# Layer 2's first normalisation in a four-layer kernel: sums of chunks 1 and 2 moved beside the first 1/std, the reciprocal in halves, seven loads in one queue

## The chip, the cores and the metric

The kernel runs on one core of a Trainium2 chip. A core has TensorE for matrix products (PE, and PEld for its loads of weights), VectorE (DVE), ScalarE (ACT) and GpSimd (POOL) for elementwise work, and SyncE (SP), which here only issues DMAs; POOL and ACT can issue DMAs too. Each engine works through its own list of instructions in order and waits on semaphores for the others. The metric is the device time of one execution in microseconds (us).

## The reference

The input x has 256 x 256 places of 128 channels. Four layers follow each other, each of the form x = x + f(gn(x)), where gn normalises groups of 4 channels over all places. Cut to what matters here:

```
# layer 1: a, b from sigmoids of products; triangle product; g * (ln(z) @ Wz + bz)
x = x + L1(gn(x))
# layer 2
zn = layernorm(gn(x))                      # over the 128 channels of each place
a = sigmoid(zn @ Wga + bga) * (zn @ Wla + bla)
b = sigmoid(zn @ Wgb + bgb) * (zn @ Wlb + blb)
k = einsum('bimc,bmjc->bijc', a, b)
x = x + sigmoid(zn @ Wgo + bgo) * (layernorm(k) @ Wlo + blo)
```

Layer 0 is a triangle attention, layer 3 a pair of small convolutions in each direction. All is in float32.

## The kernel before, in words

Activations lie in DRAM with the channels on the 128 partitions and the 65536 places along the row: `xT`, `x1T`, `x2T`, `x3T` after the layers. The places are cut into 32 chunks of `SC` = 2048, each of four pieces of `CK` = 512. Lists of instructions are as written within the blocks marked `manual_schedule`; between the blocks, instructions that touch different data may be put ahead of others of the same engine.

**Layer 1's last loop** (pool `p4`, lines 1063 to 1148) takes the 32 chunks in the order `order4`; in what follows a number between 0 and 31 in layer 1 is a place in this order. For each place, PE makes a product of the normalised z (`p4_pz`, L1116) into PSUM, which has room for one chunk only, and PE and ACT make the gate four places ahead (`gate4`, L1089 and L1092). DVE forms (pz + bz) * gate and its sum (L1126). The result is added to x either by POOL in one instruction (L1137) or, for the places in `by_dve`, by DVE in two (L1133); in that case the product stays in PSUM until the addition is done. ACT then takes the sum of squares of the new chunk (`sum4`, L1099), one place later, and SP stores it to `x2T` (L1143). `fetch_z` loads z through POOL's queue every fourth place (L1075).

**Statistics of layer 2** (lines 1155 to 1182). DVE reduces the sums, PE spreads them over groups of channels, ACT takes the square root (`gn2_sd`, L208), and DVE makes the scales: `r2`, `slide2` (a sliding column that sums channels, times r2), `mr2neg`, `wf2`, `off2`.

**Layer 2's first stage** (pool `p5`, lines 1203 to 1334). Seven chunks are loaded ahead (`load5`, L1211): chunks 0 to 3 by POOL's queue, 4 to 6 by SP's. For the layer norm over channels, ACT squares a chunk (`square5`, L1216), and PE sums the chunk and its square over channels with one-column weights (`sums5`, L1229): a group of four matmuls for x and a group of four for the squares, each on a quarter of the columns of the array; each matmul shows as two in the trace. ACT squares the mean (L1235), DVE subtracts (L1237) and clips (L1248), ACT takes the root (L1249), DVE the reciprocal. The first time this is done for chunk 0 alone: its reciprocal (L1283) is spread over the partitions by four matmuls (`broadcast_rows`, L1191) and chunk 0 is normalised by DVE from PSUM (L1290). Then it is done for chunks 1 to 3 together (`sums5(1, KB)`, L1229; reciprocal L1294), stored as a row in DRAM (L1222) and read back spread over the partitions, chunk by chunk (`spread5`, L1261). The loop over the 32 chunks (L1297) then makes four products per chunk (`product5`, L1272), two sigmoids (L1307) and two gated products (L1311), with the squares and sums for the next block of four chunks between them. PSUM pool `psM` has three buffers for the products and for the broadcast, `psX` one for the sums.

Later come layer 2's products over 128 channels (`p6`), its output (`p7`) and layer 3.

Of the kernel before, what the change touches and what calls it, by code (L numbers as in the profile page):

```python
# [8 lines left out]
F32 = mybir.dt.float32  # L9
AF = mybir.ActivationFunctionType  # L10
ALU = mybir.AluOpType
# [4 lines left out]
P = 128  # L16
# [3 lines left out]
SC = 2048  # L20
NSC = T // SC
CK = 512
# [9 lines left out]
def kernel(ctx: ExitStack, tc: tile.TileContext, a: dict, out: bass.AP):  # L32
    nc = tc.nc
# [17 lines left out]
    x2T = rows("x2T", D)  # L51
# [18 lines left out]
    const = ctx.enter_context(tc.tile_pool(name="const", bufs=1, reuse_waits="tile"))  # L70
# [30 lines left out]
    epst = const.tile([P, 1], F32, name="epst")  # L101
# [51 lines left out]
    sel = const.tile([P, 32], F32, name="sel")  # L153
# [69 lines left out]
    slide = const.tile([P, 63], F32, name="slide")  # L223
# [23 lines left out]
    with tc.tile_pool(name="x0", bufs=1, reuse_waits="tile") as xres, tc.tile_pool(name="p0", bufs=3, reuse_waits="tile") as sb:  # L247
# [14 lines left out]
        with tc.tile_pool(name="p0ps", bufs=3, space=PSUM, reuse_waits="tile") as ps, tc.tile_pool(name="f0ps", bufs=2, space=PSUM, reuse_waits="tile") as fps, tc.tile_pool(name="f0", bufs=1, reuse_waits="tile") as wk, tc.manual_schedule():  # L262
# [90 lines left out]
            for i, s in enumerate(order0):  # L353
                xt = xts.pop(s)
                xc = hold(s) if s < HELD else sb.tile([P, SC], F32, name="p0_xc", tag="xs")
                for c in range(2):
# [8 lines left out]
                    xh = xc[c] if isinstance(xc, tuple) else xc[:, c * GT : (c + 1) * GT]  # L365
# [71 lines left out]
        with tc.tile_pool(name="p1", bufs=3, reuse_waits="tile") as wk_sb, tc.tile_pool(name="p1ps", bufs=3, space=PSUM, reuse_waits="tile") as ps, tc.tile_pool(name="p1pt", bufs=2, space=PSUM, reuse_waits="tile") as psT, tc.tile_pool(name="p1mm", bufs=3, space=PSUM, reuse_waits="tile") as psP:  # L437
# [7 lines left out]
            with tc.manual_schedule():  # L445
                prs, trs, turned, sqs = {}, {}, {}, {}
# [152 lines left out]
    xs = {}  # L599
# [10 lines left out]
    with tc.tile_pool(name="p2e", bufs=6, reuse_waits="tile") as eb, tc.tile_pool(name="p2c", bufs=1, reuse_waits="tile") as cs:  # L610
        with tc.tile_pool(name="p2u", bufs=2, reuse_waits="tile") as sb, tc.tile_pool(name="p2S", bufs=2, space=PSUM, reuse_waits="tile") as psS, tc.tile_pool(name="p2z", bufs=1, space=PSUM, reuse_waits="tile") as psZ, tc.tile_pool(name="p2M", bufs=3, space=PSUM, reuse_waits="tile") as psM, ExitStack() as by_hand:
# [163 lines left out]
            for t_ in range(2):  # L775
                lo = 0 if t_ else 32
# [154 lines left out]
    with x1_scope, far_scope:  # L931
# [132 lines left out]
        with tc.tile_pool(name="p4", bufs=3, reuse_waits="tile") as sb, tc.tile_pool(name="p4psg", bufs=2, space=PSUM, reuse_waits="tile") as psg, tc.tile_pool(name="p4psz", bufs=2, space=PSUM, reuse_waits="tile") as psz, tc.manual_schedule():  # L1064
            zs, gts, sums = {}, {}, []
            junk = sb.tile([P, SC], F32, name="p4_junk", bufs=1)

            order = order4
            by_dve = (5, 11, 17, 23, 29, NSC - 1)

            def fetch_z(i):
                if i < NSC:
                    zs[i] = sb.tile([P, 2, CK], F32, name="p4_z", bufs=2)
                    for m in range(2):
                        (nc.gpsimd if i > 4 else nc.sync).dma_start(  # L1075
                            zs[i][:, m, :],
                            znD.rearrange("k (j b t) -> b j k t", j=8, t=CK)[order[i + 2 * m] % 16],
                        )

            def gate4(i):  # L1080
                if i < NSC:
                    xt = xs[order[i]]
                    tag, bufs = ("g", 3) if i % 7 < 3 else ("Z", 4)
                    gts[i] = gate_pool.tile([P, SC], F32, name="p4_g", tag=tag, bufs=bufs)
                    for h in range(2):
                        pg = psg.tile([P, 2, CK], F32, name="p4_pg")
                        for c in range(2):
                            k = 2 * h + c
                            nc.tensor.matmul(  # L1089
                                pg[:, c, :], lhsT=wgf, rhs=xt[:, k * CK : (k + 1) * CK], start=True, stop=True  # L1090
                            )
                        nc.scalar.activation(  # L1092
                            gts[i][:, h * 2 * CK : (h + 1) * 2 * CK], pg.rearrange("p c t -> p (c t)"),
                            AF.Sigmoid, bias=bgf,
                        )

            def sum4():
                i = sums.pop(0)
                nc.scalar.activation(  # L1099
                    junk, xs[order[i]], AF.Square, bias=c1neg, accum_out=qsum[:, i : i + 1]  # L1100
                )

            LEAD = 4
            fetch_z(0)
            fetch_z(4)
            for i in range(7):
                gate4(i)
            for i, s in enumerate(order):
                xt = xs[s]
                if i > 1 and i % 4 == 1:  # L1110
                    fetch_z(i + 3)
                half, z = s // 16, zs[i - i % 4]
                pz = [psz.tile([P, 2, CK], F32, name="p4_pz") for _ in range(2)]
                for c in range(4):
                    q = slice(32 * c, 32 * c + 32)
                    nc.tensor.matmul(  # L1116
                        pz[c // 2][:, c % 2, :], lhsT=wz4[q, half, :], rhs=z[q, (i // 2) % 2, :],
                        start=True, stop=True,
                    )
                if i + LEAD > 6:  # L1120
                    gate4(i + LEAD)
                gt = gts.pop(i)
                for h in range(2):
                    hs = slice(h * 2 * CK, (h + 1) * 2 * CK)
                    pzh = pz[h].rearrange("p c t -> p (c t)")
                    nc.vector.scalar_tensor_tensor(  # L1126
                        pzh if i in by_dve else gt[:, hs], pzh, bz, gt[:, hs], ALU.add, ALU.mult,
                        accum_out=usum[:, 2 * i + h : 2 * i + h + 1],
                    )
                if i in by_dve:  # L1130
                    for h in range(2):
                        hs = slice(h * 2 * CK, (h + 1) * 2 * CK)
                        nc.vector.tensor_tensor(  # L1133
                            xt[:, hs], pz[h].rearrange("p c t -> p (c t)"), xt[:, hs], ALU.add
                        )
                else:
                    nc.gpsimd.tensor_tensor(xt, xt, gt, ALU.add)  # L1137
                sums.append(i)
                if len(sums) > 1:
                    sum4()  # L1140
                if i:
                    s_ = order[i - 1]
                    nc.sync.dma_start(x2T[:, s_ * SC : (s_ + 1) * SC], xs[s_])  # L1143
                j = i - 4 + SLOTS
                if i > 3 and j < NSC:
                    load1(order[j], home[order[j - SLOTS]])
            sum4()
            nc.sync.dma_start(x2T[:, s * SC : (s + 1) * SC], xt)
# [16 lines left out]
    m2, r2 = gn_groups(mv2, "gn2")  # L1165
    wf2 = const.tile([P, 5, D], F32, name="wf2")
    nc.vector.tensor_scalar(wf2, w2[:, 0:5, :], r2, None, ALU.mult)
    slide2 = const.tile([P, 63], F32, name="slide2")
# [15 lines left out]
    H2 = 2 * CK  # L1184

    def broadcast_rows(psX, rows, s, name, tag="x"):


        rb = [psX.tile([P, 2, CK], F32, name=name, tag=tag) for _ in range(2)]
        for c in range(4):  # L1190
            nc.tensor.matmul(  # L1191
                rb[c // 2][:, c % 2, :], lhsT=sel[32 * c : 32 * c + 32, s : s + 1].to_broadcast([32, P]),
                rhs=rows[32 * c : 32 * c + 32, :], start=True, stop=True,
            )
        return [t.rearrange("p c t -> p (c t)") for t in rb]
# [7 lines left out]
    KB = 4  # L1203
    BT = KB * SC
    with tc.tile_pool(name="p5", bufs=2, reuse_waits="tile") as sb, tc.tile_pool(name="p5q", bufs=4, reuse_waits="tile") as sq_pool, tc.tile_pool(name="p5psX", bufs=1, space=PSUM, reuse_waits="tile") as psX, tc.tile_pool(name="p5psM", bufs=3, space=PSUM, reuse_waits="tile") as psM, tc.manual_schedule():
        xs, sqs, zns, vars_ = {}, {}, {}, {}

        def load5(s):
            if s < NSC:
                xs[s] = x_pool.tile([P, SC], F32, name="p5_x", tag="x")  # L1210
                (nc.gpsimd if s < KB else nc.sync).dma_start(xs[s], x2T[:, s * SC : (s + 1) * SC])  # L1211

        def square5(s):
            if s < NSC:
                sqs[s] = sq_pool.tile([P, SC], F32, name="p5_sq")
                nc.scalar.activation(sqs[s], xs[s], AF.Square, bias=mr2neg, scale=r2)  # L1216

        def store_block(dram_row, lo, hi, t):

            by_c = dram_row.rearrange("o (s c t) -> c (o s) t", c=4, t=CK)  # L1220
            for c in range(4):
                nc.sync.dma_start(by_c[c, lo:hi, :], t[32 * c + lo : 32 * c + hi, :])  # L1222

        def sums5(lo, hi):
            st = psX.tile([P, 2, CK], F32, name="p5_st")
            for s in range(lo, hi):
                for i, (w, src) in enumerate(((slide2, xs[s]), (slide, sqs[s]))):
                    for c in range(4):
                        nc.tensor.matmul(  # L1229
                            st[32 * c : 32 * c + 32, i, :], lhsT=w[:, 31 - s : 63 - s],  # L1230
                            rhs=src[:, c * CK : (c + 1) * CK], start=(s == lo), stop=(s == hi - 1),
                        )
                del sqs[s]
            mean2 = sb.tile([P, CK], F32, name="p5_m2", bufs=1)
            nc.scalar.activation(mean2, st[:, 0, :], AF.Square, bias=off2)  # L1235
            var = sb.tile([P, CK], F32, name="p5_var")
            nc.vector.tensor_tensor(var, st[:, 1, :], mean2, ALU.subtract)  # L1237
            return var
# [38 lines left out]
        for s in range(7):  # L1277
            load5(s)

        square5(0)  # L1280
        var = sums5(0, 1)
        root5(var)
        nc.vector.reciprocal(var, var)  # L1283
        store_block(rs2D, 0, 1, var)
        for s in range(1, KB):
            square5(s)
        zns[0] = sb.tile([P, SC], F32, name="p5_zn", bufs=3)
        for h, rb in enumerate(broadcast_rows(psM, var, 0, "p5_pm", tag="p5_pm")):
            hs = slice(h * H2, (h + 1) * H2)
            nc.vector.scalar_tensor_tensor(zns[0][:, hs], xs[0][:, hs], m2, rb, ALU.subtract, ALU.mult)  # L1290
        del xs[0]
        var = sums5(1, KB)
        root5(var)
        nc.vector.reciprocal(var, var)  # L1294
        store_block(rs2D, 1, KB, var)
# [771 lines left out]
```

## Time and profile before

| | us |
|---|---|
| median of 3 runs | 3239.55 (3238.77 to 3243.01) |
| the profiled execution | 3240.66 |
| its span, first to last instruction | 3238.9 |
| busy in the span: PE | 3052.9 (94%) |
| DVE | 2263.2 (70%) |
| ACT | 2034.6 (63%) |
| POOL | 1739.0 (54%) |

Layer 1's last loop runs in the trace from about 1624 to 1781 us, the opening of layer 2 from 1781 to 1811, its loop over chunks from there to about 2230. Times in the timeline are counted from the first instruction of the span. A line of the timeline gives the start, the length from the first start to the last end, engine, line, operation, what is written and read, the count of instructions merged into it, and in brackets how long the engine had been idle before and what released it.

### The profile page before, as it was taken

Reading aid. Unit: us, or ns where it says so; the run is one execution under the profiler, and the core shown is the slowest. Engines: PE = TensorE matmul, PEld = TensorE weight load, DVE = VectorE, ACT = ScalarE, POOL = GpSimd, SP = SyncE. Lnnn points to the kernel's source line nnn. Section 1 sums busy time; section 2 is a strip of 40 time slices with the busy share of each in tenths; the row PEclk is TensorE's granted clock in tenths of the full one; section 3 lists DMA queues with packets and bytes.
Section 4 is the critical chain, followed back from the end, with each engine's and each line's share of the span. In section 5 each row is a group of like instructions: output and inputs, shape, how many; then the busy total and the mean of one; then the engine's idle time right before and its main releaser. Section 6 shows DMA issues by size and latency. Waiting matters only on the chain. (4 is left out here: it accounts for less than half of the span.)

```text
span 3238.9 us, 51714 instructions
## 1 busy us (share of the span) xinstructions
PE 3052.9 (94%) x19908; PEld 1633.7 (50%) x19908; DVE 2263.2 (70%) x2630; ACT 2034.6 (63%) x2274; POOL 1739.0 (54%) x948
## 2 busy tenths in 40 slices
PE   5699999999999999998798899999999989969998
PEld 4535555555555555552533344444699933324444
DVE  5657888888888888884456454445455588858886
ACT  3576777777777777764477544443344457757776
POOL 4005777777777777771277000000255568848887
PEclk8799999999999999999999899999999999989999
DMA  9982333333333333349589677676799989976775
GB/s 372 384 317 95 106 117 118 110 113 119 113 112 120 113 106 121 117 153 420 177 313 401 232 304 296 225 284 238 280 352 351 338 324 389 389 281 197 234 235 153
DMA packets 289527, 746.19 MB, mean 230 GB/s; under 512 B 68473, under 2 KB 139019, under 8 KB 240987
## 3 DMA queue, kind: packets, MB, share of 16 engines
q1 hardware_dynamic: 277313, 720.27, 62.1%
q0 software_dynamic: 8544, 20.34, 1.7%
q8 instruction: 160, 2.62, 0.3%
q10 hardware_dynamic: 3416, 2.19, 0.3%
q14 instruction: 94, 0.77, 0.1%
HBM read 455.26 MB, written 287.45 MB: 229 GB/s over the span
## 5 line engine op out<-in xcount | busy, mean ns | idle before, releaser
L679 POOL TENSOR_TENSOR p_es<-p_e 128x1024 f32<-128x1024 f32 x256 | 603.0, 2366 | 321.2 <-DMA p_x<-xT 197.4
L669 DVE TENSOR_TENSOR p_e<-p_S,tri_raw 128x1024 f32<-128x1024 f32 x512 | 609.0, 1211 | 143.5 <-PE p_S L659 143.4
L677 ACT ACTIVATE p_e<-p_e,mbT 128x1024 f32<-128x1024 f32 x512 | 552.1, 1137 | 62.0 <-DVE p_e L669 61.9
L1272 PE MATMUL p_pm<-p_zn,wf 128*128 128x512 f32 x1040 | 448.7, 593 | 1.9 <-ACT p_a L1307 1.9
L644 PE MATMUL p_mm<-p_xn,w 128*128 128x512 f32 x764 | 404.4, 612 | 0.0
L1272 PEld LDWEIGHTS p_pm<-p_zn,wf 128*128 128x128 f32 x1040 | 196.8, 190 | 253.9 <-issue 247.0
L659 PE MATMUL p_S<-p_qk 32*128 32x256 f32 x4096 | 295.5, 400 | 3.3 <-DVE p_e L669 3.3
L1369 POOL MEMSET k<- 128x512 f32 x1 | 0.5, 527 | 520.8 <-PE p_pm L1272 520.8
L659 PEld LDWEIGHTS p_S<-p_qk 32*128 32x128 f32 x4096 | 186.0, 184 | 159.2 <-PE p_mm L635 91.7
L2025 PE MATMUL tp_z<-p_B,tp_at 128*128 128x256 f32 x1024 | 250.5, 388 | 1.0 <-DMA p_B<-bD 0.7
L692 PE MATMUL p_o<-p_e,p_vg 128*32 128x256 f32 x4096 | 248.8, 383 | 0.0
L626 POOL TENSOR_TENSOR p_xn<-p_xn,p_rs 128x1024 f32<-128x1024 f32 x62 | 148.7, 2398 | 181.1 <-DMA p_rb<-rzD 102.2
L1400 POOL TENSOR_TENSOR k<-k,p_sq 128x512 f32<-128x512 f32 x128 | 163.1, 1274 | 136.4 <-ACT p_sq L1398 136.4
L2025 PEld LDWEIGHTS tp_z<-p_B,tp_at 128*128 128x128 f32 x1024 | 185.1, 191 | 23.6 <-DVE tp_at L2016 1.7
L1399 DVE TENSOR_TENSOR k<-tp_z,k 128x512 f32<-128x512 f32 x128 | 88.6, 692 | 127.2 <-ACT p_sq L1398 127.2
L644 PEld LDWEIGHTS p_mm<-p_xn,w 128*128 128x128 f32 x764 | 125.1, 190 | 103.7 <-issue 87.3
L692 PEld LDWEIGHTS p_o<-p_e,p_vg 128*32 128x32 f32 x4096 | 120.3, 110 | 110.4 <-ACT p_vg L650 41.5
L650 ACT ACTIVATE p_vg<-p_mm,bgh 128x512 f32<-128x512 f32 x128 | 87.9, 687 | 135.2 <-PE p_mm L644 135.2
L1396 ACT COPY p_K<-tp_z 128x512 f32<-128x512 f32 x128 | 75.0, 586 | 155.1 <-PE tp_z L2025 155.1
L1311 DVE SCALAR_TENSOR_TENSOR p_b<-p_pm,b2w,p_b 128x1024 f32<-128x1024 f32 x64 | 82.1, 1283 | 123.7 <-PE p_pm L1272 109.6
L635 PEld LDWEIGHTS p_mm<-w,p_xn 128*128 128x128 f32 x1016 | 133.8, 192 | 61.3 <-issue 60.6
L648 ACT ACTIVATE p_qk<-p_mm,cqkg 128x512 f32<-128x512 f32 x127 | 87.2, 687 | 122.6 <-PE p_mm L644 122.3
(409 smaller groups left out, 6089.2 us busy)
## 6 DMA issues: line engine op xcount, KB each, us to landing
p_x<-x2T SPq DMA_DIRECT2D x60, 1024.0 KB
x<-x1T SPq DMA_DIRECT2D x47, 1024.0 KB
p_x<-in_x_dram SPq DMA_DIRECT2D x32, 1024.0 KB
p_x<-xT SPq DMA_DIRECT2D x64, 512.0 KB
p_rs<-rsD SPq DMA_DIRECT2D x64, 512.0 KB
x2T<-x SPq DMA_DIRECT2D x32, 1024.0 KB
aD<-p_a SPq DMA_DIRECT2D x32, 1024.0 KB
bD<-p_b SPq DMA_DIRECT2D x32, 1024.0 KB
```

The costliest lines, as they stand in the source:

```text
L626: nc.gpsimd.tensor_tensor(xn, xn, groups[g]["rs"], ALU.mult)
L635: nc.tensor.matmul(pm[:, k * D : (k + 1) * D], lhsT=t["xn"][:, b * P : (b + 1) * P], rhs=wf[:, 2 * D : 3 * D], start=True, stop=True,)
L644: nc.tensor.matmul(pm, lhsT=w, rhs=t["xn"][:, cs_], start=True, stop=True)
L659: nc.tensor.matmul(Ss[h // 2][:, h % 2, u, :], lhsT=t["k"][hp, r * N + u * P : r * N + (u + 1) * P], rhs=t["q"][hp, r * N : (r + 1) * N], ...
L669: nc.vector.tensor_tensor(e[:, :, 2 * p : 2 * p + 2, :].rearrange("p u h n -> p h u n"), Ss[p], triT[:, 2 * p : 2 * p + 2, :, :], ALU.add,)
L677: nc.scalar.activation(e[:, u, :, :], e[:, u, :, :], AF.Exp, bias=mbT[:, u, i : i + 1])
L679: nc.gpsimd.tensor_tensor(es, e[:, 0, :, :], e[:, 1, :, :], ALU.add)
L692: nc.tensor.matmul(t["o"][hp, r % 2, :], lhsT=t["v"][:, r * 2 + u, hp], rhs=e[:, u, h, :], start=(u == 0), stop=(u == 1),)
L1272: nc.tensor.matmul(pm[:, c, :], lhsT=wf2[:, i, :], rhs=zns[s][:, k * CK : (k + 1) * CK], start=True, stop=True)
L1399: nc.vector.tensor_tensor(k1, pz, k1, ALU.add)
L1400: nc.gpsimd.tensor_tensor(k2, k2, sq, ALU.add)
L2025: nc.tensor.matmul(pz[:, t, :], lhsT=at[:, u, t * P : (t + 1) * P], rhs=Bc[:, u, :], start=(u == 0), stop=(u == 1))
```

## The change

- `by_dve` goes from places 5, 11, 17, 23, 29, 31 to 4, 10, 16, 22, 27, 31.
- At place 28 ACT gets a small square root that nobody reads; the load of the square root's table, which stood ahead of `gn2_sd`, is placed there with it.
- All seven first loads are issued by POOL. Chunk 0's load stands ahead of the last addition of layer 1 in POOL's list, the other six after it; before it was one, then three, and three on SP.
- `sums5` is cut into `part5` (one group of four matmuls) and `close5` (from the squared mean on). Chunk 0's sums go to a buffer of `psM`.
- ACT's list is now square 0, square 1, squared mean of chunk 0, root, squares 2 and 3; before it was square 0, squared mean, root, squares 1 to 3.
- PE's list is now chunk 0's two groups, chunk 1's two, chunk 2's x, the broadcast in eight matmuls of 256 columns, chunk 3's x, chunk 2's squares, chunk 3's squares. Before, all six groups of chunks 1 to 3 stood after the broadcast, which was four matmuls of 512 columns.
- The reciprocal of chunk 0 is two instructions of 256 columns, and its normalisation four of 512 elements per partition in place of two of 1024.

No other engine's list changes in any other place.

```diff
-            by_dve = (5, 11, 17, 23, 29, NSC - 1)
+            by_dve = (4, 10, 16, 22, 27, NSC - 1)
...
+                if i + LEAD == NSC:
+                    nc.scalar.activation(const.tile([P, 1], F32, name="root_b"), epst, AF.Sqrt)
...
-                (nc.gpsimd if s < KB else nc.sync).dma_start(xs[s], x2T[:, s * SC : (s + 1) * SC])
+                (nc.gpsimd if s < 7 else nc.sync).dma_start(xs[s], x2T[:, s * SC : (s + 1) * SC])
...
+        def part5(st, s, lo, hi, i):
+            w, src = ((slide2, xs[s]), (slide, sqs[s]))[i]
+            for c in range(4):
+                nc.tensor.matmul(
+                    st[32 * c : 32 * c + 32, i, :], lhsT=w[:, 31 - s : 63 - s],
+                    rhs=src[:, c * CK : (c + 1) * CK], start=(s == lo), stop=(s == hi - 1),
+                )
...
-        square5(0)
-        var = sums5(0, 1)
+        for s in range(2):
+            square5(s)
+        st0 = psM.tile([P, 2, CK], F32, name="p5_pm")
+        st1 = psX.tile([P, 2, CK], F32, name="p5_st")
+        for i in range(2):
+            part5(st0, 0, 0, 1, i)
+        var = close5(st0)
         root5(var)
-        nc.vector.reciprocal(var, var)
+        for s in range(2, KB):
+            square5(s)
+        part5(st1, 1, 1, KB, 0)
+        part5(st1, 1, 1, KB, 1)
+        part5(st1, 2, 1, KB, 0)
+        zns[0] = sb.tile([P, SC], F32, name="p5_zn", bufs=3)
+        rb = [psM.tile([P, 2, CK], F32, name="p5_pm") for _ in range(2)]
+        Q = CK // 2
+        for w in range(2):
+            ws = slice(w * Q, (w + 1) * Q)
+            nc.vector.reciprocal(var[:, ws], var[:, ws])
+            for c in range(4):
+                nc.tensor.matmul(
+                    rb[c // 2][:, c % 2, ws], lhsT=sel[32 * c : 32 * c + 32, 0:1].to_broadcast([32, P]),
+                    rhs=var[32 * c : 32 * c + 32, ws], start=True, stop=True,
+                )
         store_block(rs2D, 0, 1, var)
-        for s in range(1, KB):
-            square5(s)
-        zns[0] = sb.tile([P, SC], F32, name="p5_zn", bufs=3)
-        for h, rb in enumerate(broadcast_rows(psM, var, 0, "p5_pm", tag="p5_pm")):
-            hs = slice(h * H2, (h + 1) * H2)
-            nc.vector.scalar_tensor_tensor(zns[0][:, hs], xs[0][:, hs], m2, rb, ALU.subtract, ALU.mult)
+        for h in range(2):
+            for w in range(2):
+                ws = slice(w * Q, (w + 1) * Q)
+                xh, zh = (
+                    t.rearrange("p (c t) -> p c t", t=CK)[:, 2 * h : 2 * h + 2, ws] for t in (xs[0], zns[0])
+                )
+                nc.vector.scalar_tensor_tensor(zh, xh, m2, rb[h][:, :, ws], ALU.subtract, ALU.mult)
         del xs[0]
-        var = sums5(1, KB)
+        part5(st1, 3, 1, KB, 0)
+        part5(st1, 2, 1, KB, 1)
+        part5(st1, 3, 1, KB, 1)
+        for s in range(KB):
+            del sqs[s]
+        var = close5(st1)
         root5(var)
```

More of the change, by code (lines that the diff above doesn't have):

```diff
@@ L1226, in sums5, with close5 @@
             for s in range(lo, hi):
[L1227 to L1232, printed above, removed]
+                part5(st, s, lo, hi, 0)
+                part5(st, s, lo, hi, 1)
                 del sqs[s]
+            return close5(st)
+        def close5(st):
             mean2 = sb.tile([P, CK], F32, name="p5_m2", bufs=1)
```

## The prediction, on record before the result

> **What bounds the kernel now.** I read the page first (PE busy 94% of the span), then the table by stretches, then the timeline, engine by engine, from 1760 to 1812 us, where the edited lines run, then the waits and the landings of the first loads. The page's chain does not reach back this far, so the local chain is followed by hand.
>
> The table of stretches: columns are length, busy time (and count) of PE, PEld, DVE, ACT, POOL, then PE clock, DMA share, GB/s.
> ```profile
> 1782.00:1795.00 13.00, 5.33 (x26) 2.09 (x30) 5.73 (x9) 7.90 (x7) 0.00 (x0) 0.50 1.01 405
> 1795.00:1811.00 16.00, 14.12 (x69) 4.37 (x70) 7.25 (x6) 8.49 (x8) 0.00 (x0) 0.86 0.27 111
> 1811.00:2230.00 419.00, 419.00 (x1308) 176.38 (x1308) 206.35 (x156) 198.45 (x163) 0.00 (x0) 1.00 0.70 262
> ```
> From 1811 PE never stops for 419 us: whatever the opening of layer 2 saves or loses moves all that follows. In 1782 to 1795 PE is busy for 5.33 of 13 us, at half clock, and DMA is full.
>
> The timeline of layer 1's end (POOL) and of the opening (ACT, DVE, PE): start, length, idle before and its releaser.
> ```profile
> 1763.88 4.53 POOL L1137 TENSOR_TENSOR x<-x,p_g 128x2048 f32<-128x2048 f32 x1 [0.64 <-DVE p_g L1126]
> 1768.34 0.58 POOL L1211 DMA_DIRECT2D p_x<-x2T  x1
> 1772.39 4.49 POOL L1137 TENSOR_TENSOR x<-x,p_g 128x2048 f32<-128x2048 f32 x1 [3.46 <-DVE p_g L1126]
> 1776.83 1.61 POOL L1211 DMA_DIRECT2D p_x<-x2T  x3
> ...
> 1779.04 2.00 ACT L1099 ACTIVATE p_junk<-x,c1neg 128x2048 f32<-128x2048 f32 x1
> 1781.16 1.28 ACT L208 ACT_TABLE_LOAD   x1
> 1782.48 0.26 ACT L208 ACTIVATE gn_sd<-gn_pv,epst 128x1 f32<-128x1 f32 x1
> 1783.84 2.09 ACT L1216 ACTIVATE p_sq<-p_x,mr2neg,gn_rstd 128x2048 f32<-128x2048 f32 x1 [1.10 <-DVE mr2neg L1173]
> 1788.62 0.69 ACT L1235 ACTIVATE p_m<-p_st,off 128x512 f32<-128x512 f32 x1 [2.68 <-PE p_st L1229]
> 1795.95 2.09 ACT L1216 ACTIVATE p_sq<-p_x,mr2neg,gn_rstd 128x2048 f32<-128x2048 f32 x1 [0.68 <-DMA p_x<-x2T]
> ...
> 1791.33 3.35 DVE L1283 RECIPROCAL p_var<-p_var 128x512 f32<-128x512 f32 x1 [0.79 <-ACT p_var L1249]
> ...
> 1786.62 1.93 PE L1229 MATMUL p_st<-p_sq,slide 128*32 128x512 f32 x8
> 1794.74 2.09 PE L1191 MATMUL p_pm<-p_var,sel 32*128 32x512 f32 x8 [6.19 <-DVE p_var L1283]
> 1796.76 1.94 PE L1229 MATMUL p_st<-p_x,slide 128*32 128x512 f32 x8
> 1799.88 1.03 PE L1229 MATMUL p_st<-p_x,slide 128*32 128x512 f32 x8
> 1803.41 5.42 PE L1272 MATMUL p_pm<-p_zn,wf 128*128 128x512 f32 x12
> 1810.72 1.55 PE L1272 MATMUL p_pm<-p_zn,wf 128*128 128x512 f32 x3 [1.89 <-ACT p_a L1307]
> ...
> DMA to landing us min/median/max: 9.1/11.4/17.9
> ```
> The path: POOL's last add (to 1776.88), two sums on ACT (to 1781.14), the group deviation (1782.48), square and sums of chunk 0, mean squared (1788.62), root, reciprocal (to 1794.68), broadcast, then six groups of sums of chunks 1 to 3 (1796.76 to 1803.41). From their end, root, a square, the sigmoid's table and the first sigmoid free PE at 1810.72, 7.3 us later. The six groups stand behind a reciprocal that they do not need: PE idles 6.19 us.
>
> [...] a group starts every 1.71 us (1796.76 to 1798.47), later every 0.86 (1799.88 to 1800.74). [...] The loads issued on POOL landed 9.1 to 17.9 us after issue while DMA was full; [...]
>
> **The change, part by part.**
>
> *Layer 1's last chunks* (numbers are places in its order). Until chunk 26 each group of six still has one chunk added by DVE; moved by one, it costs PE the same stall (chunks follow at 4.97 and 5.90 us instead of 4.70 after chunk 23), so nothing. At the end DVE adds 27 instead of 29. DVE has room at 1758.6, and its 2.35 us end at 1760.9, before the products of 28 are ready (1761.3): free. But POOL now adds 28, 29, 30 in a row: from 1763.88, two in 9.06 us, then the load's issue (0.58, 0.07 of it overlapped), then 4.49: end 1777.94 against 1776.88. Chunk 31 on DVE ends some 4 us earlier and gains nothing, as its sum is last on ACT. **+1.06 us** on the path.
>
> *Sqrt table earlier.* Its old load ended at 1782.44, when the matmul it waited with ended too (gn_sd at 1782.48): it saves 0.03. At its new place, before the sum of chunk 27, the next sum that matters waits for POOL until 1768.44: 0, and 1.3 us only if that cover went.
>
> *Chunk 1's square ahead of chunk 0's mean squared.* The group deviation is now at 1783.54, square 0 ends at 1787.0, its four matmuls at 1789.0 (1.93 and a hop; chunk 0's other sums no longer wait for off2 and are done). Square 1 (2.09) fits there if chunk 1 has landed by 1786.9. Its load issues at 1777.94; with the 9.1 us of before it lands at 1787.0. Mean squared then starts at **1789.2, +0.6** on before: 0.4 less than the +1.06, as PE's queue is shorter. Behind square 1 on ACT stand mean squared, root and all that waits for them, so each us later than 1786.9 costs 1 us.
>
> *One queue.* Chunks 4 to 6 leave SP's queue for POOL's (three issues of about 0.55 us, nothing of POOL's behind them until layer 2's products of channels). SP keeps the stores of 30 and 31, 2 MB. So chunk 1 shares with these first; 2 and 3 no longer share with 4 to 6. Bounds for chunk 1 from its issue to landing: [...] 13.4, which chunk 2 took before in second place; so mean squared at 1789.0 to 1793.4. I take the 9.1 that chunk 1 took before in the same crowd. Chunks 2 and 3 follow at some 2.6 us each, by about 1793; squares 2 and 3, after the root, end by 1796.5: hidden.
>
> *Reciprocal in halves.* Two of 256 columns cost the same 3.35 plus about 0.05; the last half ends at mean squared + 6.1 = 1795.3. The first half's broadcast lies under the second; the last four matmuls of 256 columns cost half of 2.09: 1796.35. Four normalising pieces of 512 elements (0.69 each, the PSUM subtraction of that size) end near 1798: under the sums.
>
> *Three groups of sums move ahead of the broadcast* (chunk 1's two, chunk 2's first), into the 6.19 us in which PE idled. Three stay after it: cold 3 x 1.71, warm 3 x 0.86. PE will have been busy from 1787 to about 1793, then idle some 2 us around the broadcasts, so it may be cold again. I take cold, cold, warm: 4.3 us, end 1800.7. Before: 1803.41. **Gain 2.7 us**; ends 1.9 (all cold) and 5.0 (all warm). From there the chain to the second sigmoid is unchanged, and so is chunk 1's row of 1/std (stored, spread and normalised by 1818.9, hardly ahead of PE): it moves along.
>
> Sum: span 3238.9 - 2.7 = 3236.2; the profiled execution lies 1.76 over its span (3240.66), so 3237.96; the median of the runs is 1.11 below that execution: **3236.8**.
>
> **Rivals.**
> *Warm PE:* the clock holds through the broadcasts, the three groups take 2.6. For: three groups more keep PE busy. Against: at 1767.6 PE was cold after 2.6 us idle. 5.0 us, 3234.5; 6.1 if layer 1's end also costs nothing.
> *Late chunk 1 (slower):* square 1 blocks ACT in front of mean squared. Two stores and six loads crowd the queues. It decides where chunk 1 lands after about 1789.6 (11.7 us from issue), when the 2.7 are gone; at the 13.4 us that chunk 2 took before, mean squared starts at 1793.4, loss 1.5, 3241; at 17.9 us, loss 6.0, 3245.5. Against: chunk 1 is first in its queue.
> *Nothing arrives:* the opening shrinks, but chunk 1's spread row is late by as much (its normalisation ended only some 0.4 us before PE wanted it), or a window of PE's clock falls worse: 3239.5. That the order itself does not change is excluded: the built instruction order shows it.
>
> **How the numbers follow.** Forecast 0.45 (own range 3234.5 to 3239), warm 0.25, late 0.15, nothing 0.15. 0.2% is 6.5 us, about what a measurement of this kernel can tell from no change; the shown runs differ by 4.2. Faster by more: 0.12 from warm with a favourable tail, 0.06 from the forecast's end: 0.18. Slower by more: half of late, 0.08. Within: 0.74. The range 3231.5 to 3242.5 takes warm, nothing and the near half of late, with 1.5 us for the runs' spread.
>
> **What would show it.** Right: POOL's last layer 1 add ends near 1778 with no 3.46 us wait; mean squared near 1789; groups of sums between 1789 and 1794; products from about 1800.7. Wrong: ACT's square 1 waiting for DMA past 1789; three groups at 0.86 us; the first add of the three starting elsewhere than 1763.9; PE waiting for chunk 1's normalised tile near 1816.

## The result, and the profile after

| | us | ratio to before, 95% interval |
|---|---|---|
| before | 3240.05 median (3233.81 to 3249.22, 11 runs) | |
| after | 3234.13 median (3229.0 to 3240.03, 11 runs) | 0.9981 [0.9973, 0.9989] |

The changed kernel is 0.19% faster, about 6 us. That lies in the forecast range (3231.5 to 3242.5) and within the 0.2% that had 0.74. But the forecast gain was 2.7 us, less than half of this, and the likeliest case's own range (3234.5 to 3239) just misses the median. The experiments show that the agreement is mostly luck: the 6 us come from a place that the prediction never looked at.

First the steps that it did look at. The table by stretches of the kernel after (length, busy time and count of PE, PEld, DVE, ACT, POOL, then PE clock, DMA share, GB/s):
```profile
1782.00:1795.00 13.00, 9.28 (x54) 3.32 (x54) 4.99 (x12) 8.20 (x7) 0.00 (x0) 0.73 1.01 424
1795.00:1811.00 16.00, 13.31 (x57) 4.90 (x50) 9.57 (x10) 10.24 (x8) 0.00 (x0) 0.85 0.30 124
1811.00:2230.00 419.00, 419.00 (x1306) 176.22 (x1305) 205.57 (x156) 196.08 (x162) 0.00 (x0) 1.00 0.71 262
```
The stretch in which PE had been busy for 5.33 us now has 9.28: the idle time is filled as meant. The timeline of the same kernel, POOL, ACT, DVE and PE:
```profile
1763.32 9.02 POOL L1139 TENSOR_TENSOR x<-x,p_g 128x2048 f32<-128x2048 f32 x2 [7.89 <-DVE p_g L1128]
1772.88 4.53 POOL L1139 TENSOR_TENSOR x<-x,p_g 128x2048 f32<-128x2048 f32 x1
1777.34 3.19 POOL L1213 DMA_DIRECT2D p_x<-x2T  x6
...
1783.01 0.26 ACT L208 ACTIVATE gn_sd<-gn_pv,epst 128x1 f32<-128x1 f32 x1 [1.34 <-PE gn_pv L206]
1787.14 2.10 ACT L1218 ACTIVATE p_sq<-p_x,mr2neg,gn_rstd 128x2048 f32<-128x2048 f32 x1 [0.69 <-DMA p_x<-x2T]
1789.97 0.69 ACT L1244 ACTIVATE p_m<-p_pm,off 128x512 f32<-128x512 f32 x1 [0.73 <-PE p_pm L1229]
...
1792.68 3.36 DVE L1307 RECIPROCAL p_var<-p_var 128x256 f32<-128x256 f32 x2 [0.79 <-ACT p_var L1258]
...
1797.27 1.94 PE L1229 MATMUL p_st<-p_x,slide 128*32 128x512 f32 x8
1798.97 2.02 PE L1229 MATMUL p_st<-p_sq,slide 128*32 128x512 f32 x16
1800.93 5.42 PE L1281 MATMUL p_pm<-p_zn,wf 128*128 128x512 f32 x12
1808.23 4.30 PE L1281 MATMUL p_pm<-p_zn,wf 128*128 128x512 f32 x6 [1.89 <-ACT p_a L1342]
```
Products of chunk 0 start at 1800.93 (forecast 1800.7, before 1803.41). But two pieces of PE's work on the way fall in large part into a half-clock stretch in this profile, which they did not before: eight gate matmuls at 1754.17 take 5.37 us (3.67 before; granted clock 0.50 from 1754.86 to 1758.27), and six products after 1808.23 take 4.30 (three took 1.55 before; 0.50 from 1809.47 to 1812.89). At the last product of the layer the changed kernel leads by only 0.8 us (2301.20 against 2301.99), and at layer 3's start by 0.1 (2877.03 against 2877.10). The rest of the gain arises in layer 3, whose code is untouched. From its last root of statistics to the start of its last product it takes 344.3 us, against 348.4.

Where layer 3 waits, by groups of instructions in its steady part (2960 to 3180 us): the second product by `w2c` on PE, and DVE's sum of the loaded taps. The last field is the engine's idle time ahead of the group and what ended it. Before:
```profile
L1739 PE MATMUL p_pm<-p_pb,w2c 128*128 128x512 f32 x176 | 79.9, 597 | 5.0 <-DVE p_pb L1747 4.8
L1647 DVE TENSOR_REDUCE p_acc<-p_S 128x41 f32<-128x369 f32 x11 | 9.0, 816 | 8.8 <-DMA p_S<-sD 8.8
```
After:
```profile
L1774 PE MATMUL p_pm<-p_pb,w2c 128*128 128x512 f32 x184 | 83.3, 595 | 2.1 <-DVE p_pb L1782 2.0
L1682 DVE TENSOR_REDUCE p_acc<-p_S 128x41 f32<-128x369 f32 x11 | 9.0, 818 | 5.6 <-DMA p_S<-sD 5.6
```
A load of layer 3 arrives earlier, though nothing was done to it.

### The profile page after: what moved, and what is told of

Same layout as the page of the kernel before. It is cut to its first block, busy times and chain, and to the rows that moved or that the text cites. A ratio compares the mean times of both kernels' runs of the same rounds, so it can differ in the third digit from the quotient of the medians.

```text
span 3233.8 us, 51742 instructions
## 1 busy us (share of the span) xinstructions
PE 3052.5 (94%) x19916; PEld 1629.4 (50%) x19916; DVE 2266.3 (70%) x2633; ACT 2035.2 (63%) x2275; POOL 1742.1 (54%) x951
## 5 line engine op out<-in xcount | busy, mean ns | idle before, releaser
L626 POOL TENSOR_TENSOR p_xn<-p_xn,p_rs 128x1024 f32<-128x1024 f32 x62 | 148.9, 2402 | 180.7 <-DMA p_rb<-rzD 119.6
```

Source lines behind the costliest of these rows:

```text
L626: nc.gpsimd.tensor_tensor(xn, xn, groups[g]["rs"], ALU.mult)
```

## Experiments: does the gain belong to the edit?

Four kernels on one chip (before: 3235.47 us there). Two are the kernels themselves again, to see how far profiles of one program differ.

> The kernel before, unchanged, for a second profile and as a null comparison. In the first pair of profiles layer 0's first addition stood at 250.54 us before and 246.68 after, though nothing there was edited. If that is chance from execution to execution: it lies anywhere between 246 and 251 here, ratio 1.000 within its interval. If it comes from the changed program: 250.5 again, within 0.5. The local stretch, from DVE's first gated product of place 4 to PE's release by the first sigmoid of layer 2 (168.48 us before, 169.89 after), should be 168.5 within 0.3 if it is a property of the program, and spread by 1.7 or more if phases of PE's clock decide it.

> The changed kernel again. Theory of the opening: products of chunk 0 begin 19.5 to 20 us after the last sum of squares of layer 1 ends (19.36 in the first profile after, 22.27 before). Theory of chance elsewhere: layer 0's first addition anywhere between 246 and 251 us, the wait of PE for the load of place 31 (1.98 us in the first profile) gone or small in some runs, and the cold window of PE in chunk 0's products (1.70 us) in some runs only. Theory of a displaced memory map: 246.7 again.

The third adds to the kernel before only the constant that the changed kernel adds, without the root:
```diff
                 if i + LEAD > 6:
                     gate4(i + LEAD)
+                if i + LEAD == NSC:
+                    const.tile([P, 1], F32, name="root_b")
```


> The kernel before with one unused tile of four bytes per partition among the constants. The new small tile of the change displaces 2246 of the other tiles in SBUF by 32 bytes; here 2262 are displaced by the same, and nothing else changes. If the displacement is what made the rest of the kernel faster: 3 to 4 us faster than before, layer 0's first addition near 246.7. If not: ratio 1.000, 246 to 251 as it falls.

The fourth is the changed kernel without that tile; its root goes into the tile of the early sigmoid (named `sigmoid_a` at its creation):
```diff
-                    nc.scalar.activation(const.tile([P, 1], F32, name="root_b"), epst, AF.Sqrt)
+                    nc.scalar.activation(sigmoid_a, epst, AF.Sqrt)
```


> The changed kernel with its small root written into an old tile of the constants that is no longer needed, so that no tile is displaced. If the displacement carries part of the gain: 3 to 4 us slower than the changed kernel, at or above the kernel before in the local stretch alone. If not: the same as the changed kernel, some 3 to 6 us faster than before.

The ratios here and below are taken over all runs of a kernel against those of the kernel before on the same chip; they are not the quotients of the medians. The column on layer 3 is from one profile each.

| | median us | ratio, 95% interval | layer 3, us |
|---|---|---|---|
| before_again | 3237.81 | 1.0006 [0.9998, 1.0014] | 350.7 |
| after_again | 3231.91 | 0.9987 [0.9979, 0.9995] | 343.7 |
| shift_only | 3232.45 | 0.9986 [0.9979, 0.9994] | 341.7 |
| after_no_shift | 3235.86 | 1.0004 [0.9995, 1.0013] | 347.7 |

An unused tile gives the whole gain, and the change without it gives none that can be measured. Of the theories on record the displaced memory map stands; the opening, and chance elsewhere, don't explain the pattern. In the built programs that tile takes 32 bytes of each partition, and everything allocated after it in SBUF lies 32 bytes further on: 2262 allocations. (The changed kernel's profile led by 3.9 us already in layer 0; before_again, which is the kernel before, did so by 4.0. That part is difference between executions: over all fourteen profiles of this document layer 0's first addition lies between 245.8 and 250.7 us, and the profiles with and without the displacement overlap.)

Some of what was expected did not come. The local stretch of before_again was 168.9 us, outside 168.5 by more than the 0.3 allowed, while the eight profiles with the old order in layers 1 and 2 spread by 1.1 us, not by 1.7. In after_again the products began 18.6 us after the last sum of squares, ahead of the 19.5 to 20 expected; PE's wait for the load of place 31 (1.45 us) and the half-clock window in chunk 0's products came again, so these two weren't rare chances of the first profile.

## Experiments: which tile, and which address?

In the trace's packet records one size stands out. Layer 3's output tile `p9_o` is stored in rows of 512 bytes. The 65,872 packets of that size (65,536 of them are its rows) took 29.6 ns on average before and 27.4 after; 6.4% of them took 41 ns before, 0.04% after. `p9_o` starts at byte 211424 of the partition before, 224 past a multiple of 256 (and its second buffer likewise), and at 211456 after, a multiple of 512. Five kernels move it. The unused tile of shift_only made larger (16 and 24 words):

> The kernel before with one unused tile of 64 bytes (instead of 32 as in shift_only) in the constant pool at the same place: everything that lay 32 bytes past a multiple of 64 lies there again, 64 bytes further on. Theory 'address of the rows' (the 512-byte packets of layer 3's output store read SBUF rows that start 32 bytes past a multiple of 64 in the kernel before, 0 past one in the displaced kernels): no gain, ratio to before 0.9995 to 1.0010; 512-byte packets at 29.4 to 29.7 ns as before, layer 3 (last root of its statistics to its last product) 347 to 351 us. Theory 'any displacement': ratio 0.998 to 0.999 as shift_only had.

> The kernel before with one unused tile of 96 bytes: the output tile starts at a multiple of 64 but 64 past a multiple of 512 (shift_only: a multiple of 512). If 64 bytes are what counts: ratio 0.998 to 0.999, 512-byte packets at 27.2 to 27.6 ns, layer 3 at 341 to 345 us. If rows of 512 bytes must start at a multiple of 512: ratio about 1.000 and packets near 29.5 ns, layer 3 at 347 to 351 us.

And an unused tile directly ahead of `p9_o`, which moves nothing else (1 word for 32 bytes, 40 words for 160, 72 for 288):
```diff
         def emit(s):
             qf = qs.pop(s).rearrange("p h w -> p (h w)")
+            if s == 0:
+                sb.tile([P, 1], F32, name="pad", bufs=1)
             ot = sb.tile([P, SC // P, D], F32, name="p9_o")
```


> The kernel before with an unused 32-byte tile directly ahead of layer 3's output tile: the two buffers of the output tile alone move by 32 bytes, every other tile stays. Theory 'output store': the whole gain of shift_only, ratio 0.998 to 0.999, 512-byte packets 27.2 to 27.6 ns, layer 3 at 341 to 345 us. Rival 'loads of layer 3' (the rows of taps, the chunks of x, the tap rows written out, whose tiles stay where they are): ratio about 1.000, layer 3 at 347 to 351 us, whatever the packets of the store do.

> As o_only, but the two buffers of the output tile start 256 past a multiple of 512. If a multiple of 512 is needed: packets with a tail at 41 ns as in pad96 (about 6 in 100), ratio 0.9995 to 1.0005. If a multiple of 256 is enough: 98 in 100 packets at 27 ns and ratio 0.9978 to 0.9988.

> As o_only, but the two buffers start 128 past a multiple of 512. If a multiple of 128 is enough: 98 in 100 packets at 27 ns and ratio 0.9978 to 0.9988; if more is needed: packets as in pad96 and ratio 0.9995 to 1.0005.

Before was 3236.03 us on the chip of the first three, 3235.45 on that of o_256 and o_128. "Rate" is that of the last output store at the end of the program, where no other large transfer of the program is left; "tail" runs from the start of the last product by `w2c` to the end of the span. A tile is called on the grain below where it starts at a multiple of 256 bytes, and off it elsewhere.

| | `p9_o` past a multiple of 256, of 512 | packets, mean ns | at 41 ns | rate GB/s | tail us | layer 3 us | ratio, 95% interval |
|---|---|---|---|---|---|---|---|
| before | 224, 480 | 29.6 | 6.4% | 293 | 13.3 | 348.4 | |
| pad64 | 32, 32 | 28.1 | 6.3% | 292 | 13.3 | 348.8 | 0.9997 [0.9989, 1.0005] |
| pad96 | 64, 64 | 27.9 | 6.0% | 293 | 13.3 | 350.6 | 1.0002 [0.9994, 1.0010] |
| o_128 | 128, 128 | 29.0 | 6.3% | 293 | 13.3 | 347.1 | 1.0004 [0.9994, 1.0014] |
| o_256 | 0, 256 | 27.2 | 0.01% | 348 | 12.3 | 343.0 | 0.9985 [0.9977, 0.9993] |
| o_only | 0, 0 | 27.4 | 0.03% | 348 | 12.2 | 341.8 | 0.9979 [0.9971, 0.9987] |
| shift_only | 0, 0 | 27.2 | 0.01% | 348 | 12.3 | 341.7 | 0.9986 [0.9979, 0.9994] |
| after | 0, 0 | 27.4 | 0.04% | 348 | 12.4 | 344.3 | 0.9981 [0.9973, 0.9989] |

o_only gives the full gain with two buffers of one tile moved, so the rival "loads of layer 3" falls. pad64 and pad96 give nothing, so the theory "any displacement" falls, and so does my first guess that 64 bytes are the grain. o_128 against o_256 puts it at 256 bytes. The packets of pad64, pad96 and o_128 were expected near 29.5 ns; their mean is lower, but the tail at 41 ns is there.

The rate at which the last store runs can be read straight from the stretches of 2 us after the last instruction of PE: columns as above, the last two the DMA share and GB/s. Before:
```profile
3233.53:3235.53 2.00, 0.00 (x0) 0.00 (x0) 0.00 (x0) 0.00 (x0) 0.00 (x0) 0.50 1.08 293
```
After:
```profile
3229.35:3231.35 2.00, 0.00 (x0) 0.00 (x0) 0.00 (x0) 0.00 (x0) 0.00 (x0) 0.52 1.15 348
```
pad96, o_128, o_256, o_only:
```profile
3228.53:3230.53 2.00, 0.00 (x0) 0.00 (x0) 0.00 (x0) 0.00 (x0) 0.00 (x0) 0.71 0.93 293
```
```profile
3235.05:3237.05 2.00, 0.00 (x0) 0.00 (x0) 0.00 (x0) 0.00 (x0) 0.00 (x0) 0.77 1.00 293
```
```profile
3220.28:3222.28 2.00, 0.00 (x0) 0.00 (x0) 0.00 (x0) 0.00 (x0) 0.00 (x0) 0.93 1.15 348
```
```profile
3224.93:3226.93 2.00, 0.00 (x0) 0.00 (x0) 0.00 (x0) 0.00 (x0) 0.00 (x0) 1.00 1.15 348
```
All compute engines are idle in each, and the store has the DMA engines to itself; the rate is 293 or 348, nothing between (pad64: 292). The lengths of the packets are a mark of the grain and not what makes the rate. In these stretches (and that of pad64) some 1,160 packets start off the grain and 1,360 on it, and off it at most 12 of them took 38 ns or more; in pad96 their mean is 25.8 ns, below the 27.0 of the kernels on the grain, and yet the rate is 293.

All four offsets off the grain, 32, 64, 128 and 224 bytes, give one rate, 292 to 293. Why rows that start there are stored more slowly was not shown.

What it is worth, by an estimate from the two rates: the layer stores 33.6 MB, 114.5 us of full DMA at 293 GB/s and 96.4 at 348, 18 us less in a layer of some 350. Where it reaches the end: about 1.1 us in the tail (13.3 to 12.2 in the kernel before, 13.5 to 12.4 in the changed one), and the rest ahead of the last product. In the stretch 2960 to 3180 us DVE's two sums wait for the loads of taps for 8.7 to 15.2 us in the seven profiles with `p9_o` off the grain, and for 1.9 to 7.9 in six of the seven with it on the grain (9.4 in the seventh, opening_only, whose layer 3 is also slow at 349.6; that execution took 4.9 us more than the median of its kernel). PE's wait for the second product, which follows, is 3.5 to 7.6 against 0.0 to 2.3 (5.2 in opening_only). I read this as the faster stores letting the small loads of taps land sooner. It rests on these waits, whose two ranges nearly meet; whether the loads queue behind the stores in SP's list or on the DMA engines wasn't separated. Over all runs the mean ratio is 1.0002 for the six timings off the grain and 0.9983 for the seven on it: 0.19% of 3236, about 6 us, which is the whole difference between the two kernels of this case.

## Experiments: what the parts of the change do

With the tile's displacement held fixed, the shares of layer 1 and the opening of layer 2 can be looked at alone. New opening with the old shares, displaced and not displaced, and the new shares alone, displaced:
```diff
-            by_dve = (4, 10, 16, 22, 27, NSC - 1)
+            by_dve = (5, 11, 17, 23, 29, NSC - 1)
```
(in the changed kernel: opening_only; in after_no_shift: opening_no_shift; the reverse in shift_only: shares_only)

> The changed kernel with layer 1's old shares (DVE's chunks 5, 11, 17, 23, 29, 31), the displacement kept. Theory 'place 31's load': without the later store of place 18 the wait of PE for that load is back at 0.4 to 0.6 us and its half-clock matmuls are gone; place 28 to the first product of chunk 0 stays 39.5 to 41.5 us (41.8 to 42.1 before), place 4 to place 28 loses up to 3 us against the changed kernel's profile; ratio 0.9975 to 0.9985. Rival 'the shares are worth their 1.06 us and the wait costs nothing on average': ratio 0.9985 to 0.9995, no better than the changed kernel.

> The new opening of layer 2 alone: old shares of layer 1, and no tile displaced (the early root is written into the tile of the early sigmoid). Theory 'the opening gains 2.5 us': place 28 to the first product of chunk 0 at 39.0 to 40.5 us where PE's clock holds, up to 41.5 where the six groups fall into a half-clock window; ratio 0.9987 to 0.9998. Theory 'nothing arrives': the start of the products gains, but the ratio is 0.9998 to 1.0006, and the lost part shows between the first and the last product of the layer (498.6 us in the kernel before).

> The kernel before, displaced as in shift_only, with the change's new shares of layer 1 alone (DVE adds chunks 4, 10, 16, 22, 27, 31). The prediction's step says +1.06 us at layer 1's end: from place 28's first gated product to the first group deviation of layer 2 22.2 to 22.3 us instead of 21.1 to 21.2, to the first product of chunk 0 42.8 to 43.6 us instead of 41.8 to 42.4; PE's wait for place 31's load 1.0 to 2.0 us (0 to 1.6 with the old shares). Ratio to before 0.9988 to 0.9996, that is 1 to 3 us above shift_only. Rival 'the shares pay': ratio 0.998 to 0.9986.

Marks in each profile, us. "28" is the first gated product of place 28 in layer 1; the deviation is `gn2_sd`; the products are those of chunk 0.

| | place 4 to 28 | 28 to deviation | to mean squared | to products | sum from 28 | place 4 to layer 2's last product | ratio, 95% interval |
|---|---|---|---|---|---|---|---|
| before | 119.06 | 21.18 | 6.13 | 14.80 | 42.11 | 659.74 | |
| seven others with old shares and opening | 118.59 to 120.22 | 21.18 to 22.14 | 6.00 to 6.14 | 14.27 to 15.17 | 41.76 to 43.18 | 659.46 to 660.55 | |
| forecast for after | as before | 22.24 | 5.66 | 11.5 | 39.4 | | |
| after | 122.40 | 22.27 | 6.96 | 10.96 | 40.19 | 662.86 | 0.9981 [0.9973, 0.9989] |
| after_again | 120.08 | 22.26 | 7.73 | 9.49 | 39.48 | 659.82 | 0.9987 [0.9979, 0.9995] |
| after_no_shift | 119.64 | 22.26 | 6.73 | 12.54 | 41.52 | 659.74 | 1.0004 [0.9995, 1.0013] |
| opening_only | 119.36 | 21.19 | 7.34 | 11.13 | 39.66 | 657.60 | 0.9979 [0.9973, 0.9986] |
| opening_no_shift | 119.15 | 21.18 | 7.52 | 11.13 | 39.84 | 657.56 | 0.9998 [0.9990, 1.0007] |
| shares_only | 119.62 | 22.25 | 5.89 | 14.22 | 42.36 | 660.55 | 0.9986 [0.9978, 0.9993] |

The opening alone gains 2.45 us up to the last product (657.58 against a mean of 660.03 of the eight with the old order), in both profiles alike. In the full change the three profiles stand at 662.86, 659.82 and 659.74, a mean of 660.81: nothing is left of it on average. The timings can't resolve 2.45 us (0.08%); opening_no_shift at 0.9998 fits both it and none, and its layer 3 happened to be the longest of all (351.1). shares_only equals shift_only in the timings, and its 0.9986 lies at the edge of the rival's range ("the shares pay") and outside my own (0.9988 to 0.9996). The 1.07 us at its deviation isn't visible there, and only partly at its products (42.36, where 42.8 to 43.6 was expected), since mean squared and sums took less in that profile. opening_only met its numbers but for the wait for place 31's load (0.73 us, 0.4 to 0.6 expected), and its interval reaches the rival's. So the timings don't settle what the new shares cost. opening_only and o_only, at 0.9979, are the fastest versions, but neither stands clear of the changed kernel's 0.9981 and 0.9987.

## Why the prediction was right, point by point

The range and the likeliest verdict held. Most terms of the local sum held too, but what they gained was on average lost again in the same two layers, and the term that made the measured gain was missing.

- *Layer 1's last chunks, +1.06.* Right: POOL's last add ends 16.66 or 16.67 us after place 28's product in the four profiles with the new shares, and 15.58 in the kernel before, 1.08 less (15.6 in eight of the ten profiles with the old shares, 15.9 in shift_only, 16.5 in pad64). The clause "moved by one, so nothing" is less sure. The store of place 18 is later because POOL now adds it next to 17, and its buffer takes place 31's load; PE waited 0.98 to 1.98 us for that load (old shares: 0 to 1.58, 0.43 before; opening_only 0.73). In the profile after, where the wait was longest, a half-clock window followed, eight matmuls took 1.7 us more, and place 4 to 28 took 122.4 us; in the three other profiles with the new shares (119.6 to 120.1) it is inside the spread of the old ones.
- *Sqrt table earlier, 0.* Right: the deviation comes 22.25 us after place 28 with the table at its old place (shares_only) and 22.26 at the new one.
- *Mean squared at 1789.2.* It started 1.1 to 2.1 us later than worked out. Chunk 1 was not the cause: it landed 8.5 to 9.8 us after its issue in the five profiles with the new opening (9.1 assumed; that POOL's loads and SP's transfers share the DMA shows in the kernel before, where the two queues moved 2.09 and 2.10 MB between 1784 and 1794), and the 0.7 us that square 1 waited in three of them lay inside the time that PE took anyway. *Late chunk 1* did not occur. The step that failed is "chunk 0's other sums no longer wait for off2 and are done". ACT's list in opening_only shows it: both squares end by 1786.06, and mean squared waits for PE.
```profile
1781.98 4.08 ACT L1218 ACTIVATE p_sq<-p_x,mr2neg,gn_rstd 128x2048 f32<-128x2048 f32 x2 [1.10 <-DVE mr2neg L1175]
1787.96 0.69 ACT L1244 ACTIVATE p_m<-p_pm,off 128x512 f32<-128x512 f32 x1 [1.90 <-PE p_pm L1229]
```
  PE's list shows why. In the kernel before, the small product for `off2` came first, and then chunk 0's four matmuls of x ran side by side in 1.93 us, at a granted clock of 0.50 too:
```profile
1784.10 0.56 PE L1177 MATMUL f_o<-mr2neg,ones 128*128 128x1 f32 x2
1784.91 1.93 PE L1229 MATMUL p_st<-p_x,slide 128*32 128x512 f32 x8 [0.25 <-DVE off L1178]
```
  In opening_only the small product stands behind the first of these four, which takes 1.91 us alone (so does the one at 1784.68 in after, at a granted clock of 0.50); the other three start only after the small product, with the squares' sums.
```profile
1782.30 1.91 PE L1229 MATMUL p_pm<-p_x,slide 128*32 128x512 f32 x2
1784.14 0.59 PE L1179 MATMUL f_o<-mr2neg,ones 128*128 128x1 f32 x2
1784.65 1.07 PE L1229 MATMUL p_pm<-p_x,slide 128*32 128x512 f32 x3
```
  The list of the change and the prediction both missed that one instruction had moved past another. No run put it back, so that it alone makes the delay is read from these lists.
- *Three groups moved ahead of the broadcast, 1.9 (cold) to 5.0 (warm).* Right, with the guess "cold, cold, warm" in the middle: from the start of the groups after the broadcast to the products it took 3.7 us in after (1797.27 to 1800.93, forecast 4.3), 2.7 in after_again and 5.2 in after_no_shift, whose two last groups took this:
```profile
1795.38 3.60 PE L1230 MATMUL p_st<-p_sq,slide 128*32 128x512 f32 x16
```
  Against 2.02 in after: all of cold, mixed and warm occurred in three executions of the same order. In the kernel before, the prediction's 1.71 us a group was taken at a granted clock of 0.50 and its 0.86 at 1.00, with the change at 1799.57. The stretches between recorded changes of the clock in the traces are multiples of 3.41 us but for one or two in a trace (47 of 48 in before and in after, from 3.41 to 1174.18 us), and where they lie against the work differs from execution to execution: full clock came back 2.8 us after the start of the groups behind the broadcast in before, 2.0 in after. Below, a window is a step of 3.41 us counted from the recorded changes.
- *Reciprocal in halves.* The two halves took 3.36 us (3.40 forecast). In the profile after, the normalising pieces started only after the last broadcast and ended at 1800.09, not near 1798, but still ahead of the products.
- *"From there the chain is unchanged."* Wrong in two profiles of three. The same 1.9 us wait for the first sigmoid stands in all, but in after and after_again a half-clock window then fell on chunk 0's products: first to last product 500.27 and 500.26 us, against 498.57 in the twelve others. That is the *Nothing arrives* rival's second clause, at 1.7 us. In both the wait lies wholly inside one window (in after it runs from 1806.34 to 1808.23, the window from 1806.06 to 1809.47); in eleven others the end of a window cuts it (in before 1808.83 to 1810.72, cut at 1809.81). In opening_only it lies inside one as well and the clock held, so this isn't all that decides. An idle gap of 1.9 us, shorter than a window, was followed by half clock here. Counted in the same way over the fourteen traces, with PE's idle time as recorded, all 241 full-clock windows with more than 2.05 us idle were followed by half clock, 3 of the 11,880 with less than 1.15 us were, and between the two both occur (before and after alone: 35 of 35, and 1 of 1,696).
- *The sum.* The forecast 2.7 us at the start of the products was 0.6 to 2.6 from place 28 on (41.52 to 39.48 against 42.11), and about nothing on average at the last product. The measured 6 us came from a line that the prediction costed only as a table load and that also allocates a tile. The *Warm PE* rival named nearly the right time (3234.5) for a reason that held in only one profile of the changed kernel.

None of the cases held a gain from another layer.

## What to carry to other kernels

An edit that adds even a 4-byte tile moved what is allocated after it here: before a small gain or loss is put down to the edit's logic, time the kernel before with that tile alone, and the edit without it. Give a tile that is stored in rows of 512 bytes a start that is a multiple of 256 bytes; here this one displacement was worth 0.19% of the whole kernel, more than the reordering that came with it. When work is moved ahead on PE's list, list every small matmul that it now passes: with one matmul of 1.91 us, at half clock, in front of the product for `off2`, the time from the deviation to mean squared grew by 0.6 to 1.6 us, where the forecast shortened it by 0.5.

## What the runs showed of the hardware that I had not expected

- A store from SBUF in 512-byte rows ran at 348 GB/s with rows at multiples of 256 bytes and at 292 to 293 with rows 32, 64, 128 or 224 past one.
- Off the grain some 6% of the packets took 41 ns, against 0.01 to 0.04% on it.
- The rate did not follow the recorded length of the packets: 293 GB/s at a mean of 25.8 ns in pad96's last store, 348 at 27.0 on the grain.
- One and the same idle gap of 1.9 us on PE was followed by a half-clock window, which cost 1.7 us, in the two executions of the changed kernel, and not in after_no_shift, which has the same order. In these traces more than 2.05 us of idle time inside one full-clock window of 3.41 always brought half clock after it (241 of 241), and less than 1.15 almost never (3 of 11,880); in this count a gap that a window's end cuts in two adds to each window only its part.
